# A two-layer graph kernel: small constants and later Wqk chunks on GpSimd's queue, pair 0's softmax in other space, and the last pair transposed by TensorE

## The chip, the core and the metric

The kernel runs on one core of a Trainium2 chip. TensorE (PE) does the matrix products, VectorE (DVE) and ScalarE (ACT) the elementwise work, GpSimd (POOL) and SyncE (SP) mostly start DMA transfers. The metric is the device time of one execution in microseconds. Before the change it is 2383.96 us, the median of 3 runs (2383.9 to 2384.36).

## What is computed

There are 128 independent graphs of 128 nodes with 512 features, all in float32. Two layers follow each other, each with a layer norm, a ReLU and a residual:

```python
# layer 0: h = relu(layernorm(x))
e = leaky_relu(sj[:, None, :] + si[:, :, None] + ab[0], 0.2)   # sj, si: projections of h
transition = A * exp(e) / (sum(A * exp(e), -1) + 1e-12)
H = sum over k of (Xk @ Wk[k] + bk[k]);  Xk = transition @ Xk    # k = 0, 1, 2
x = x + relu(H)
# layer 1: h = relu(layernorm(x))
q, k = split(h @ Wqk, 2);  v = h @ Wv
w = inv_scale * mask * sum(q * (adj @ (k * mask)), -1)
x = x + softmax(w, axis=nodes)[:, :, None] * v
```

## The kernel before

The graphs go through in 64 pairs (G = 2). Weights stay in SBUF. Both layers' products are seven Strassen products over blocks of the two graphs and two halves of the features (`strassen0`, lines 408 to 443, and `strassen1`, lines 445 to 472), so that the two large matrix products take 7/8 of the plain multiplications. Sums of weight blocks (`combine`, lines 193 to 199) are made once, sums of activation blocks (`left_sums`, line 385) once a pair. In layer 1, q never exists: `score_matrix` (lines 222 to 246) makes M = Wq Wk^T from eight chunks of Wqk that TensorE first transposes, four steps o = 0 to 3 with two chunks each.

The main loop (line 555) is a software pipeline over pairs. In turn p it runs layer 0's products of pair p, the propagation of pair p+1 (`propagate`, line 373), the norms of layer 1 for pair p and of layer 0 for pair p+2, layer 1's products of pair p-1, and the transpose of pair p's layer-1 input h2. A scheduler then orders each engine's instructions; an engine works through its own queue strictly in that order. At most eight transfers that SP and ACT start, and eight that GpSimd starts, are in flight, since each takes one of eight semaphores in turn and waits for the transfer that had it before.

The activations must stand transposed for the products. The kernel does this through memory: `by_blocks` (lines 296 to 304) writes h to DRAM (`hd`) and reads it back in 32-row blocks (`hv`), and `transposed` (line 306) lets DVE transpose 32x32 blocks, so that the features come in a permuted order (f, c, a) which the weights' rows follow.

The softmax over a graph's nodes needs the score column w as a row on all partitions. `spread_pair` (lines 312 to 327) does it by two small DMAs on GpSimd's queue (`pwd`, then `pw`), or for the last pair by TensorE (`spread`, line 115). `finish` (lines 492 to 510) then takes the maximum, the exponentials and the final multiply-add, and stores the pair. `end` (line 551) calls it for the pair before, in the middle of `strassen0`; in the last turn (p = 64), where there is no `strassen0`, it is called first of all (line 566), ahead of the last pair's layer-1 products.

At the start (lines 516 to 547) the norm of pair 0, the loading of pair 1, the row sums of Wv (`wv0_sums`, line 139), five small constants on SP's queue (lines 519 to 523), the score matrix, the layer-0 weight blocks (`stacked_weights`, line 204), the first attention and the first propagation follow each other. All eight Wqk chunks are started from ACT's queue (line 122), and `attention(0, ...)` uses the one-buffer tile `junk`, in which also every multiply-and-accumulate of DVE leaves its unwanted product.

Of the kernel before, what the change touches and what calls it, by code (L numbers as in the profile page):

```python
# [8 lines left out]
FP = mybir.dt.float32  # L9
AF = mybir.ActivationFunctionType  # L10
OP = mybir.AluOpType
# [4 lines left out]
def kernel(  # L16
# [55 lines left out]
    def load_x(p):  # L72
        s = slice(p * G, (p + 1) * G)
        xg[p] = loads.tile([P, G, D], FP, name="xg")
        nc.sync.dma_start(xg[p], x[s].rearrange("b n d -> n b d"))
        ag[p] = loads.tile([P, G, N], FP, name="ag")
        nc.sync.dma_start(ag[p], adj[s].rearrange("b n m -> n b m"))

# [37 lines left out]

        nc.tensor.transpose(dst, col.to_broadcast([P, P]), ident)

    def wqk_chunk(a, o):
        w = wpool.tile([P, DC, P], FP, name=f"w{a}")  # L120
        at = a * D + o * P
        nc.scalar.dma_start(w, wqk[:, at:at + P].rearrange("(c p) o -> p c o", p=P))
        return w

    nc.scalar.dma_start(awr, aw.rearrange("n o -> o n"))
    wchunks = {0: [wqk_chunk(a, 0) for a in range(2)]}
    for c in range(DC):
        nc.sync.dma_start(wv0_sb[c], wv0[c * P:(c + 1) * P])
    wchunks[1] = [wqk_chunk(a, 1) for a in range(2)]


    u_bc = const.tile([P, 2, D], FP, name="u_bc")
# [65 lines left out]
        nc.vector.tensor_sub(t[3], b21, t[1])  # L198
        return dict(zip((5, 6, 7, 4, 1, 2, 3), t + [b11, b21, b22]))

    bsum = const.tile([P, D], FP, name="bsum")
    blocks0, right0 = {}, {}

    def stacked_weights():
        blocks0["b11"] = block0(const, "b11", 0, 0)
        blocks0["b12"] = block0(None, "b12", 0, 1)
        blocks0["b22"] = block0(const, "b22", 1, 1)
        blocks0["b21"] = block0(const, "b21", 1, 0)

    def bias():  # L210
        pb = ps_t.tile([P, D], FP, name="pt")
# [10 lines left out]
    def score_matrix(o):  # L222

        if o == 0:
            pms.extend(ps_m.tile([P, D], FP, name="pm") for _ in range(DC))
        ws = wchunks.pop(o)
        wt = []
        for a in range(2):
            p = ps_t.tile([P, DC, P], FP, name="pt")
            for c in range(DC):  # L230
                nc.tensor.transpose(p[:, c, :], ws[a][:, c, :], ident)
            t = wpool.tile([P, D], FP, name=f"wt{a}")
            if a:
                nc.scalar.copy(t, p.rearrange("p c i -> p (c i)"))
            else:
                nc.scalar.copy(t.rearrange("p (f c a) -> p f c a", f=Q, c=DC),
                               p.rearrange("p c (f a) -> p f c a", f=Q))
            wt.append(t)
        if o + 2 < DC:
            wchunks[o + 2] = [wqk_chunk(a, o + 2) for a in range(2)]  # L240
        for c in range(DC):
            nc.tensor.matmul(pms[c], wt[0][:, c * P:(c + 1) * P], wt[1],
                             start=(o == 0), stop=(o == DC - 1))
            if o == DC - 1:
                for nh in range(2):
                    nc.scalar.copy(e[c // HC, nh][:, c % HC, 0, :], pms[c][:, nh * HD:(nh + 1) * HD])


    def norm_relu(src, name, pool):

        mv = small.tile([P, G, 2], FP, name="mv")
        for j in range(G):
# [13 lines left out]
        nc.vector.scalar_tensor_tensor(rs[:, 1], mean, -1.0, rs[:, 0], op0=OP.mult, op1=OP.mult)  # L266
        h = pool.tile([P, G, D], FP, name=name)
        for j in range(G):
            nc.scalar.activation(h[:, j, :], src[:, j, :], AF.Relu,  # L269
                                 bias=rs[:, 1, j:j + 1], scale=rs[:, 0, j:j + 1])  # L270
        return h

    cols = [const.tile([P, S32], FP, name=f"col{i}") for i in range(6)]
    for t in cols:
# [31 lines left out]
    def transposed(hv, dst):  # L306

        for j in range(G):
            nc.vector.transpose(dst[:, j].rearrange("p f (n b) -> p f n b", n=Q),  # L309
                                hv[:, j].rearrange("p n (f a) -> p f n a", f=Q))  # L310

    def spread_pair(col, name, by_dma):

# [131 lines left out]
    def strassen1(p, ahead):  # L445

        product = products(SX2.pop(p), R1)
        X2.pop(p)
        yv = late["p"].tile([P, G, 2, 2, HD], FP, name="yv")
        o = [[yv[:, j, nh].rearrange("p k d -> p (k d)") for nh in range(2)] for j in range(G)]  # L450
        s = late["p"].tile([P, 3, D], FP, name="s1")
        a, b, c = (ps_m.tile([P, D], FP, name="pm") for _ in range(3))
        product(a, 1, True)
        nc.scalar.copy(s[:, 0], a)
        product(b, 6, True)
        nc.vector.tensor_add(s[:, 1], b, s[:, 0])  # L456
        product(c, 7, True)
        agg = [aggregate(p, 0)]
        product(b, 5, False)
        nc.vector.tensor_add(s[:, 2], b, s[:, 0])  # L460
        nc.vector.tensor_add(o[1][1], c, s[:, 2])
        if ahead < NP:
            score_sums(ahead)
        product(a, 2, False)
        nc.scalar.copy(o[0][0], a)
        agg.append(aggregate(p, 1))
        H2.pop(p), AT.pop(p)
        product(b, 3, False)
        nc.vector.tensor_add(o[0][1], b, s[:, 0])
        product(c, 4, False)  # L470
        nc.vector.tensor_add(o[1][0], c, s[:, 1])
        return yv, scores(p, yv, agg)

    def aggregate(p, j):

        pa = ps_t.tile([P, D], FP, name="pt")
        nc.tensor.matmul(pa, AT[p][:, j, :], H2[p][:, j, :], start=True, stop=True)  # L477
        return pa

    def scores(p, yv, agg):  # L480

        w = cols[3 + p % 3]
        for j in range(G):
            junk = front.tile([P, D], FP, name="junk", bufs=1)
            b = p * G + j
            nc.vector.scalar_tensor_tensor(
                junk.rearrange("p (k d) -> p k d", k=2), agg[j].rearrange("p (k d) -> p k d", k=2),
                wscale[:, b:b + 1], yv[:, j, :, 0, :], op0=OP.mult, op1=OP.mult,
                accum_out=w[:, j:j + 1])
        return w  # L490

    def finish(peak, p, yv, ws, pw):


        w = ws[:, :6 * G].rearrange("p (k g) -> p k g", g=G)
        nc.vector.tensor_reduce(peak, pw, AX.X, OP.max, negate=True)
        for j in range(G):
            ej = front.tile([P, N], FP, name="ej")
            nc.scalar.activation(ej, pw[:, j, :], AF.Exp, bias=peak[:, j:j + 1],
                                 accum_out=w[:, 2, j:j + 1])  # L500
        nc.vector.tensor_add(w[:, 3], w[:, 0], peak)
        nc.scalar.activation(w[:, 4], w[:, 3], AF.Exp)
        nc.vector.reciprocal(w[:, 5], w[:, 2])
        nc.vector.tensor_mul(w[:, 3], w[:, 4], w[:, 5])
        x1 = X1.pop(p)
        for j in range(G):
            o = x1[:, j, :].rearrange("p (k d) -> p k d", k=2)
            nc.vector.scalar_tensor_tensor(o, yv[:, j, :, 1, :], w[:, 3, j:j + 1], o,  # L508
                                           op0=OP.mult, op1=OP.add)
        nc.sync.dma_start(out[p * G:(p + 1) * G].rearrange("b n d -> n b d"), x1)  # L510

    def begin(p):
        X[p] = front.tile([P, K, G, 2, HC, N], FP, name="x")
        transposed(HV.pop(p), X[p][:, 0].rearrange("p j h c n -> p j (h c) n"))

    norm0(0)
    load_x(1)
    wv0_sums()
    nc.sync.dma_start(bvc, bv0.rearrange("(p c) -> p c", c=DC))
    nc.sync.dma_start(awc, aw.rearrange("(a p c) o -> p a (c o)", a=2, c=DC))  # L520
    nc.sync.dma_start(ab_bc, bcast(ab, 0, 1))
    nc.sync.dma_start(bsum[:K], bk)
    nc.sync.dma_start(nm, nodemask)
    score_matrix(0)
    stacked_weights()
    score_matrix(1)
    attention_weights()
    masks()
    score_sums(0)
    score_matrix(2)  # L530
    attention(0, front.tile([P, D], FP, name="junk", bufs=1)[:, :G * N])
    score_matrix(3)
    bias()
    t_transposed(0)
    begin(0)
    propagate(0)
    prepare0(0)
    right0.update(combine(t=[const.tile([P, K, HC, HD], FP, name=f"t{i}") for i in range(1, 5)],
                          **blocks0))
    load_agb(0, X[0][:, 1, 0, 0, 0, 0:1])  # L540
    load_agb(1)
    transposed_adj(0)
# [12 lines left out]
    for p in range(NP + 1):  # L555
        if p < NP:
# [5 lines left out]
            strassen0(p, steps)  # L562
            if p + 1 < NP:
                propagate(p + 1)
        else:
            end()
        if p == 0:
            right1.update(combine(e[0, 0], e[0, 1], e[1, 0], e[1, 1], f))
            setup_ctx.close()
            R1 = {i: t.rearrange("p (s c) k o -> p s c (k o)", s=1) for i, t in right1.items()}  # L570
            late["p"] = ctx.enter_context(tc.tile_pool(name="late", bufs=1))
        if p < NP:
            H2[p] = norm_relu(X1[p], "h2", late["p"])
            hv2 = by_blocks(H2[p])
        if p + 2 < NP:
            norm0(p + 2)
        if p > 0:
            yv, w = strassen1(p - 1, p + 2)
        elif p + 2 < NP:
            score_sums(p + 2)  # L580
        if p + 1 < NP:
            prepare0(p + 1)
        if p > 0:
            ends.append((p - 1, yv, w, spread_pair(w, "pw", p < NP)))
        if p < NP:
            X2[p] = late["p"].tile([P, G, 2, HC, N], FP, name="x2")
            transposed(hv2, X2[p].rearrange("p j h c n -> p j (h c) n"))
            a = {(j, kh): X2[p][:, j, kh:kh + 1].rearrange("p k c n -> p k (c n)")
                 for j in range(G) for kh in range(2)}
            SX2[p] = left_sums(a, late["p"], "sx2", [1, HD])  # L590
    end()


# [23 lines left out]
```

## Time and profile before

| what | value |
|---|---|
| median time | 2383.96 us |
| span of the profiled execution | 2381.4 us |
| PE busy | 2343.4 us (98%) |
| DVE busy | 1828.5 us (77%) |
| ACT busy | 637.7 us (27%) |
| POOL busy | 374.3 us (16%) |
| DMA | 243.93 MB, mean 102 GB/s |

PE is busy in all but 38 us of the span. The page's second part, busy tenths in 40 slices, has PE at 9 in every slice but the first (8) and the last (6). The waits of PE in the first 80 us and in the last 40 us are views to read beside it, and the timeline around them. Two things help in reading. A wait is put down to the instruction that came last; behind a DVE instruction there may be another that held DVE's queue. And a matrix product of 128x512 in float32 is two records 0.43 us apart when the clock is full, so 0.86 us.

### The profile page before, as it was taken

How to read it: one execution, taken by the hardware profiler on the slowest of the kernel's cores; microseconds unless marked ns; L12 is line 12 of the kernel's file. 1: busy time of each engine (PE TensorE's matmuls, PEld its weight loads, DVE VectorE, ACT ScalarE, POOL GpSimd, SP SyncE). 2: the span in 40 equal slices, each digit the busy share in tenths (PEclk: the TensorE clock that was granted, in tenths of full speed). 3: DMA queues.
4: the chain of work that ended last, by engine and by line, in shares of the span. 5: the costliest groups of instructions: out<-in, count | busy, mean ns of one | idle time of the engine just before them, and what ended most of it. 6: DMA issues, size and time to landing. Idle time of an engine off the chain costs nothing.

```text
span 2381.4 us, 27851 instructions
## 1 busy us (share of the span) xinstructions
PE 2343.4 (98%) x8921; PEld 1660.8 (70%) x8921; DVE 1828.5 (77%) x4956; ACT 637.7 (27%) x1560; POOL 374.3 (16%) x653
## 2 busy tenths in 40 slices
PE   8999999999999999999999999999999999999996
PEld 5677677677677676676776776776776776766763
DVE  6787787887877877877877877878878778778764
ACT  3222222222222322322222222222223223223221
POOL 3111111111111111111111011111111111111100
PEclk9999999999999999999999999999999999999998
DMA  7334334344344344344343343343343443443421
GB/s 209 96 86 115 102 94 107 99 105 107 96 108 107 85 119 105 83 117 110 84 116 108 88 107 104 100 107 101 103 107 97 107 107 89 115 106 81 108 69 47
DMA packets 257357, 243.93 MB, mean 102 GB/s; under 512 B 28821, under 2 KB 182549, under 8 KB 257209
## 3 DMA queue, kind: packets, MB, share of 16 engines
q1 hardware_dynamic: 230150, 213.00, 31.6%
q0 software_dynamic: 22832, 27.05, 6.4%
q10 hardware_dynamic: 4226, 2.10, 0.3%
q8 instruction: 70, 1.15, 0.2%
q14 instruction: 79, 0.64, 0.1%
HBM read 141.25 MB, written 100.79 MB: 102 GB/s over the span
## 4 chain that ended last, share of the span: by engine, by line
PE 90%; DVE 3%; DMA 2%; issue 1%; ACT 0%; POOL 0%; DVEq 0%; POOLq 0%; ACTq 0%
PE pm L402 75%; PE pt L381 8%; PE pt L477 4%; PE pt L369 1%; DMA pwd<-pwt 1%; PE pt L365 1%; DMA pw<-pwd 1%; DVE st L254 0%; DMA pz<-pzd 0%; DVE junk L292 0%; DMA pzd<-pzt 0%; DVE x L309 0%; DVE x L442 0%; DVE x L508 0%; DVE sx L390 0%
## 5 line engine op out<-in xcount | busy, mean ns | idle before, releaser
L402 PE MATMUL pm<-t,sx 128*128 128x256 f32 x2304 | 507.9, 379 | 3.4 <-DVE sx L389 3.4
L402 PEld LDWEIGHTS pm<-t,sx 128*128 128x128 f32 x2304 | 437.6, 190 | 63.7 <-DVE sx L389 4.2
L402 PE MATMUL pm<-b,x 128*128 128x256 f32 x1536 | 363.0, 379 | 0.0
L402 PE MATMUL pm<-f,sx 128*128 128x512 f32 x768 | 353.1, 595 | 1.7 <-DVE s L456 1.6
L402 PEld LDWEIGHTS pm<-b,x 128*128 128x128 f32 x1536 | 282.1, 190 | 59.6 <-issue 29.7
L320 POOL DMA_DIRECT2D pzd<-pzt x124 | 69.0, 559 | 1411.1 <-DVE pzt L317 1411.0
L402 PEld LDWEIGHTS pm<-f,sx 128*128 128x128 f32 x768 | 146.1, 191 | 187.1 <-issue 162.7
L402 PE MATMUL pm<-e,x 128*128 128x512 f32 x512 | 243.2, 597 | 13.5 <-DVE x L309 13.5
L383 ACT COPY x<-pt 128x512 f32<-128x512 f32 x256 | 147.6, 577 | 367.8 <-PE pt L381 367.7
L381 PE MATMUL pt<-tt,h 128*128 128x256 f32 x1024 | 231.6, 379 | 0.5 <-ACT tt L370 0.5
L292 DVE SCALAR_TENSOR_TENSOR junk<-h,u_bc 128x512 f32<-128x512 f32 x256 | 177.2, 692 | 66.3 <-ACT h L269 52.9
L381 PEld LDWEIGHTS pt<-tt,h 128*128 128x128 f32 x1024 | 194.5, 190 | 27.5 <-ACT tt L370 1.1
L402 PE MATMUL pm<-b,sx 128*128 128x256 f32 x768 | 176.2, 379 | 0.0
L402 PE MATMUL pm<-t,x 128*128 128x256 f32 x768 | 176.2, 379 | 0.0
L402 PEld LDWEIGHTS pm<-e,x 128*128 128x128 f32 x512 | 97.6, 191 | 110.4 <-issue 91.0
L309 DVE STREAM_TRANSPOSE x<-hv 128x512 f32<-128x512 f32 x256 | 166.3, 688 | 5.6 <-DMA hv<-hd 3.7
L337 ACT ACTIVATE s<-s 128x256 f32<-128x256 f32 x63 | 26.3, 417 | 511.3 <-DVE s L335 511.3
L402 PEld LDWEIGHTS pm<-b,sx 128*128 128x128 f32 x768 | 145.9, 190 | 19.8
L402 PEld LDWEIGHTS pm<-t,x 128*128 128x128 f32 x768 | 145.9, 190 | 19.8
L87 POOL DMA_DIRECT2D agb<-in_adj_dram x256 | 153.3, 603 | 21.1 <-issue 13.1
L269 ACT ACTIVATE h<-xg,rs 128x512 f32<-128x512 f32 x128 | 97.3, 808 | 173.7 <-DVE rs L266 173.7
L477 PE MATMUL pt<-h,aT 128*128 128x512 f32 x256 | 130.6, 592 | 0.0
(131 smaller groups left out, 2807.6 us busy)
## 6 DMA issues: line engine op xcount, KB each, us to landing
hd<-h SPq DMA_DIRECT2D x128, 512.0 KB, 4.0
hv<-hd SPq DMA_DIRECT2D x512, 128.0 KB, 5.3
xg<-in_x_dram SPq DMA_DIRECT2D x64, 512.0 KB, 3.6
out_dram<-x SPq DMA_DIRECT2D x64, 512.0 KB, 2.8
ag<-in_adj_dram SPq DMA_DIRECT2D x64, 128.0 KB, 2.7
agb<-in_adj_dram POOLq DMA_DIRECT2D x256, 32.0 KB, 4.0
pw<-pwd POOLq DMA_DIRECT2D x63, 128.0 KB, 3.3
pz<-pzd POOLq DMA_DIRECT2D x62, 128.0 KB, 5.6
```

What stands on the lines that cost most here:

```text
L87: nc.gpsimd.dma_start(agb[p][c * S32:(c + 1) * S32].rearrange("p g q i -> p (g q) i"), v[c])
L269: nc.scalar.activation(h[:, j, :], src[:, j, :], AF.Relu, bias=rs[:, 1, j:j + 1], scale=rs[:, 0, j:j + 1])
L292: nc.vector.scalar_tensor_tensor(junk, h[:, j, :], 1.0, u_bc[:, a, :], op0=OP.mult, op1=OP.mult, accum_out=s[:, a * G + j:a * G + j + 1])
L309: nc.vector.transpose(dst[:, j].rearrange("p f (n b) -> p f n b", n=Q), hv[:, j].rearrange("p n (f a) -> p f n a", f=Q))
L320: nc.gpsimd.dma_start(d[j], t[j::S32])
L337: nc.scalar.activation(ex, z, AF.Exp)
L365: nc.tensor.transpose(pt[:, j, :], t[:, j, :], ident)
L369: nc.tensor.matmul(pt[:, j, :], t[:, j, :], tt[:, j, 0, :], start=True, stop=True)
L381: nc.tensor.matmul(pt[:, c].rearrange("p k n -> p (k n)"), h[:, j, at:at + P], tt[:, j].rearrange("p k n -> p (k n)"), start=True, stop=True)
L383: nc.scalar.copy(X[p][:, 1:3, j, kh].rearrange("p k c n -> p c k n"), pt)
L402: nc.tensor.matmul(bank[:, :r.shape[-1]], left[i][:, k, c * P:(c + 1) * P], r, start=(first and at == 0), stop=(at == len(chunks) - 1), sk ...
L477: nc.tensor.matmul(pa, AT[p][:, j, :], H2[p][:, j, :], start=True, stop=True)
```

## The change

Five edits go together.

1. **Loads at the start.** The five small constants (bv, aw as columns, ab, the biases, the node mask) are started from GpSimd's queue at the very beginning instead of from SP's queue. The Wqk chunks of steps 2 and 3 also go to GpSimd's queue. Pair 0's adjacency is loaded after Wv.
2. **Order at the start.** Pair 1's x is loaded, and so normed, later: between layer 0's blocks b22 and b21 instead of ahead of `wv0_sums`. The blocks b12, b22 and b21 are loaded after the first score sums in the program's order.
3. **Space.** `attention(0, ...)` works in a corner of two not yet written weight sums (now one tile `tw`) instead of `junk`.
4. **The last pair's transpose.** Its h2 is written unpermuted by ACT, and TensorE transposes it with eight 128x128 transposes into PSUM, copied out by ACT (graph 0) and DVE (graph 1). The products that read h2 directly take it through a permuted view.
5. **The last turn.** `end` for pair 62 moves into `strassen1(63)`, behind its fourth product. The last pair is scored, finished and stored graph by graph, the first graph ahead of the seventh product in the program.

```diff
@@ load_x
-        ag[p] = loads.tile([P, G, N], FP, name="ag")
-        nc.sync.dma_start(ag[p], adj[s].rearrange("b n m -> n b m"))
+        if p > 0:
+            load_ag(p)
@@ setup
-    wchunks = {0: [wqk_chunk(a, 0) for a in range(2)]}
+    wchunks = {0: [wqk_chunk(a, 0, nc.scalar) for a in range(2)]}
     for c in range(DC):
         nc.sync.dma_start(wv0_sb[c], wv0[c * P:(c + 1) * P])
+    load_ag(0)
+    nc.gpsimd.dma_start(bvc, bv0.rearrange("(p c) -> p c", c=DC))
+    nc.gpsimd.dma_start(awc, aw.rearrange("(a p c) o -> p a (c o)", a=2, c=DC))
+    nc.gpsimd.dma_start(ab_bc, bcast(ab, 0, 1))
...
+    nc.gpsimd.dma_start(bsum[:K], bk)
+    nc.gpsimd.dma_start(nm, nodemask)
+    wchunks[1] = [wqk_chunk(a, 1, nc.scalar) for a in range(2)]
@@ score_matrix
-            wchunks[o + 2] = [wqk_chunk(a, o + 2) for a in range(2)]
+            wchunks[o + 2] = [wqk_chunk(a, o + 2, nc.gpsimd) for a in range(2)]
@@ new
+    def transposed_by_pe(h, dst):
...
+        for j in range(G):
+            pt = ps_t.tile([P, DC, P], FP, name="pt")
+            for f in range(Q):
+                nc.tensor.transpose(pt[:, f, :], h[:, j, f * P:(f + 1) * P], ident)
+            (nc.vector.tensor_copy if j else nc.scalar.copy)(dst[:, j], pt)
@@ strassen1
         nc.vector.tensor_add(o[1][1], c, s[:, 2])
...
+        if p == NP - 1:
+            end(s[:, 2, :G])
         product(a, 2, False)
...
+        w = cols[3 + p % 3]
+        if p == NP - 1:
+            last(p, yv, w, agg, 0)
         product(c, 4, False)
         nc.vector.tensor_add(o[1][0], c, s[:, 1])
-        return yv, scores(p, yv, agg)
+        if p == NP - 1:
+            last(p, yv, w, agg, 1)
+            return
...
+    def last(p, yv, w, agg, j):
...
+        score(p, yv, w, agg, j)
+        pw = ps_t.tile([P, DC, P], FP, name="pt")
+        spread(pw[:, j, :], w[:, j:j + 1])
+        finish(small.tile([P, G], FP, name="peak"), p, yv, w, pw[:, :G], slice(j, j + 1))
@@ setup order
     norm0(0)
-    load_x(1)
     wv0_sums()
-    nc.sync.dma_start(bvc, bv0.rearrange("(p c) -> p c", c=DC))
...
     score_matrix(0)
-    stacked_weights()
+    blocks0["b11"] = block0(const, "b11", 0, 0)
     score_matrix(1)
     attention_weights()
     masks()
     score_sums(0)
+    blocks0["b12"] = block0(None, "b12", 0, 1)
+    blocks0["b22"] = block0(const, "b22", 1, 1)
+    load_x(1)
+    blocks0["b21"] = block0(const, "b21", 1, 0)
     score_matrix(2)
-    attention(0, front.tile([P, D], FP, name="junk", bufs=1)[:, :G * N])
+    tw = const.tile([P, 4, K, HC, HD], FP, name="t")
+    at = K * HC * HD - N
+    attention(0, tw.rearrange("p i k c o -> p (i k c o)")[:, at:at + G * N])
@@ main loop
-            H2[p] = norm_relu(X1[p], "h2", late["p"])
-            hv2 = by_blocks(H2[p])
+            H2[p] = norm_relu(X1[p], "h2", late["p"], p == NP - 1)
+            if p + 1 < NP:
+                hv2 = by_blocks(H2[p])
...
-            transposed(hv2, X2[p].rearrange("p j h c n -> p j (h c) n"))
+            hT2 = X2[p].rearrange("p j h c n -> p j (h c) n")
+            if p + 1 < NP:
+                transposed(hv2, hT2)
+            else:
+                transposed_by_pe(H2[p], hT2)
```

## The prediction

> **What bounds the kernel now.** First the page: PE is busy 2343.4 of 2381.4 us, and in the chain that ended last 90% is PE. So every engine but PE matters only where PE waits for it, and all of PE's idle time is 38 us. The busy tenths put it at the two ends. I then read the waits of PE at each end, and the chain of the last 60 us.
>
> The waits of PE (us in total, times, longest), first from 0 to 80 us, then from 2340 us to the end:
>
> ```profile
> PE pm L402 <- DVE sx L389: 3.4, 2, 2.7
> PE pt L117 <- DVE junk L292: 2.9, 1, 2.9
> PE pt L143 <- DMA f<-in_L_gnn_aw_dram: 2.4, 1, 2.4
> PE pt L231 <- DMA w<-in_L_gnn_Wqk_dram: 1.6, 1, 1.6
> PE pt L117 <- DVE junk L148: 1.1, 1, 1.1
> PE pm L242 <- ACT wt L234: 1.0, 1, 1.0
> ...
> PE pm L402 <- DVE x L309: 11.4, 1, 11.4
> ```
>
> At the end one wait stands out: the last pair's first product waits 11.4 us for DVE's transpose of the block-wise copy `hv`. The chain over that stretch (start, us, what) shows what held DVE:
>
> ```profile
> 2345.60 0.22 DVE pwt L317
> ...
> 2346.10 0.56 POOL pwd L320
> 2346.66 2.85 DMA pwd<-pwt
> ...
> 2350.07 3.19 DMA pw<-pwd
> ...
> 2353.74 0.89 ACT ej L499 x4
> ...
> 2356.53 0.63 DVE x L309
> 2357.16 0.04 issue
> 2357.20 14.97 PE pm L402 x28
> ```
>
> It is not only the round trip of h2. `hv` was started from 2345.03 to 2346.83 and lands a median 5.3 us later (DMA issues), about 2352. But pair 62's finish stands ahead of the transpose in DVE's queue and waits for its own two DMAs until 2353.28. Both waits must go, and the change touches both.
>
> At the start, DVE and ACT are what PE waits for, and the timeline shows what they wait for:
>
> ```profile
> 13.16 1.29 DVE L254 BATCH_NORM_STATS2 st<-xg 128x6 f32<-128x512 f32 x2 [4.69 <-DMA xg<-in_x_dram]
> 16.48 0.59 ACT L236 COPY wt<-pt 128x512 f32<-128x512 f32 x1 [5.64 <-DMA ag<-in_adj_dram]
> 19.04 0.17 DVE L159 SCALAR_TENSOR_TENSOR awc<-awc,bvc 128x4 f32<-128x4 f32 x1 [3.99 <-DMA awc<-in_L_gnn_aw_dram]
> ```
>
> DVE loses 4.7 us to pair 1's x and 4.0 us to a small constant (10.1 us from issue to landing). ACT loses 5.6 us because it is itself starting Wqk chunks (its DMA issues last from 10.68 for 5.76 us) with PSUM copies queued behind.
>
> **What the Trainium skill says.** (1) "TensorE: Matmul & The Clock Gate", Part 1: after an idle window of about 3.4 us PE runs at half clock, and needs about 3.4 us of work to get back. The trace agrees: after the 11.4 us wait the weight loads come 0.85 us apart instead of 0.43. (2) Same page, Part 4: a PE transpose does 128x128 at once into PSUM, a copy must follow, and transposes don't count as work for the clock. The trace shows the duration (273 ns median at L365, 0.11 us apart), not the last. (3) "DMA: Bandwidth & Descriptors", Anatomy of one DMA: about 2 us fixed, whatever the size. Here `pwd`, with almost no bytes, took 2.85 us. (4) "Trainium Kernel Development and Optimization", Key Constraints: queues of SP, ACT and POOL share the same 16 DMA engines; another queue saves only issue time. So part 1 can move waits, not bytes; DMA is 84%, over 100% and 92% busy in the first three windows of 10 us.
>
> **The end, step by step** (in the clock of before; PE's order is read from the built program: pair 62's product 4, eight transposes, aggregate of graph 0, products 1, 6, 7, 5, 2, aggregate of graph 1, products 3, 4).
> - Pair 62's product 4 gives way to the next at 2343.88. h2 is ready earlier (ACT 2340.65 + 1.52). Eight transposes at 0.11 us: 0.9 (at half clock 1.9; I take 0.9). PE to 2344.8.
> - Aggregate 0.86, product 1 two matmuls, 1.72: to 2347.4. ACT's copy of graph 0 (0.59, as other PSUM copies) ends about 2345.1 and is hidden.
> - DVE's copy of graph 1 is no row of before; DVE's nearest PSUM read of 128x512 is 0.69, bounds 0.6 to 0.75. It is queued behind the scores of pair 62, so 2345.6 to 2346.3, then `pwt` 0.2 and three sums of 0.43: 2347.85. Product 6 waits about 0.5 us.
> - Products 6, 7, 5, 2: 6.9, aggregate 0.86, products 3 and 4: 3.4. PE ends at 2359.1. Before, DVE took up the last product at 2372.19, that is 13.1 us later. Of these 11.4 are the wait and some 2.6 the half clock after it (six matmul records 0.43 longer), less the transposes.
> - Unpermuted writing of h2 and permuted reading of h2 by two aggregates: ACT's copies with 32-element runs (L236, 586 ns) cost what plain ones do (L234, 589 ns), so 0 for ACT, hidden anyway. No row shows PE reading so; 0 to 1.7 us (a doubling), I take 0.
> - Added wait: pair 62's finish now stands in DVE's queue after product 5. `pwt` is 0.7 later, so `pw` is there at 2354.0; DVE comes to it at 2354.7 (product 5 ends 2353.1, two adds). ACT's exponentials stand behind the copy of product 2 (2355.0 to 2355.6) and end about 2356.7; two multiply-adds of 0.7 end at 2358.5. Behind them wait product 3's add and score 0 (0.69 + 0.75) and only then product 4's add: about 2360.0 instead of 2359.1. So 0.9 us of the gain goes here.
> - Tail: before, from that add (2372.19) to the last multiply-add's end (2377.33) 5.1 us. Now add, max of graph 0 (0.26), score 1 (0.75), spread 0.35, max 0.26, exponentials 0.8, graph 0's multiply-add in their shadow, small steps 0.4, graph 1's 0.7: about 4.5 us, to 2364.5. The store was 4.07 us from there to the end; half the bytes, by the loads of 128 and 512 KB (2.7 and 3.6 us) 0.4 less: 3.7. End 2368.2.
> - Sum: 2381.4 - 2368.2 = 13.2 us, bounds 11.5 (double reads, half-clock transposes) to 14.2 (no queueing at 62's finish).
>
> **The start, step by step.**
> - ACT no longer starts chunks, so the wt copies of step 1 come at about 12 instead of 16.48. PE's wait of 1.0 goes: step 1's products end 20 instead of 21.2.
> - DVE's eight row sums (0.75 each) start at 7.77 and no longer have the two waits: about 15 instead of 23.5. u_bc is ready at about 21.4 (before 26.97), score 0 at 21.8, and PE's waits of 1.1 and 2.9 shrink to about 0.3. The clock also stays up. PE reaches the transposes of t at about 33 instead of 39.4.
> - But pair 1's norm (BN 1.3, small steps), and the sums of weights (4 x 1.75), are still DVE's, now between t (about 28) and the first activation sums. Four score sums of pair 1 are put between these (0.75 each), and ACT's copies of the propagation wait for its norm. I get the second sum at 43.7 (before 48.07). So 4.4 us there, not 6.
> - Pair 1's attention then comes after the score sums and one 1.2 us weight sum, t at 53.3, while PE is there at 51.7: 1.6 back. The later waits (2.7 at L389, 2.1 at L309 near 91 us) stay: they are DVE's work per turn, not what was moved. Net 2.9 us, bounds 0.5 and 6 (all of PE's advance kept).
> - Constants on GpSimd: five issues of about 0.6 us at 1 to 5 us, behind them the chunks of step 2, the gate of b11, the chunks of step 3 and the other six Wk loads, each waiting for the one eight before. Even with 10 us of landing awc is there at 12; its instructions stand third in DVE's queue, behind them the other six row sums, which would then end at 16.5 instead of 15, still ahead of PE's 20. Wk's last blocks start at about 17 instead of 12.5 and are used at 30 and later: 0. The new space of `attention(0)`: frees DVE's `junk`, 0 by itself.
> - Steady state: each engine's order is the same for pairs 2 to 61, so 0.
>
> **Sum.** 13.2 + 3.0 = 16.2; 2383.96 - 16.2 = 2367.7 us.
>
> **Rivals.**
> - R1, the start gives nothing: DVE or a late load takes the place of the waits removed. For: DVE is 75 to 90% busy from 20 to 40 us, and DMA is full until 30. Against: 8.7 us of DVE's idle time there are pure waits. Only the end is kept: 2383.96 - 13.2 = 2370.8.
> - R2, PE's whole advance at the start is kept: 2383.96 - 13.2 - 6 = 2364.7. Against: pair 1's norm must still be done by DVE ahead of the same sums.
> - R3, slower: the five small transfers land one after another at 10.1 us each, since all chunks and Wk loads queue behind them on GpSimd. The mask would come near 52 us, where PE wants it at 24: 2383.96 + 28 - 13.2 = 2398.8. Against: before, three of them in flight together took 10 us together.
> - R4, no difference: the finish of pair 62 inside the last turn meets late DMAs and puts PSUM copies off by some 9 us: 2383.96 - 13.2 + 9 = 2379.8. Against: `pw` has 8.4 us between its transpose and its use, where before 7.7 were needed.
>
> **Chances.** As worked out 0.70, R1 0.15, R2 0.11, R3 0.02, R4 0.02. So faster 0.96, same 0.02, slower 0.02. The range takes in R1 and R2 with the bounds of the costs at the end: 2363.0 to 2372.2.
>
> **What would show it.** Right: PE has no wait over 1 us after 2340 us; the last matmul ends about 13 us earlier from the span's end of before, less the start's gain; pair 62's max sits after product 5's adds; awc is waited for by under 2 us; the first `sx`-wait of PE is over at about 44 us. Wrong: a wait of PE for `hv`'s successor x, aggregates longer than 0.86, GpSimd's chunks landing after 23 us, or other times in the middle pairs.

## The result, and the profile after

| kernel | median us | lowest to highest | ratio to before, 95% interval |
|---|---|---|---|
| before | 2384.16 | 2381.78 to 2389.9 (6 runs) | 1 |
| changed | 2366.66 | 2365.77 to 2370.26 (6 runs) | 0.9925 [0.9913, 0.9938] |

The change takes 17.5 us off. 2367.7 was predicted, between 2363.0 and 2372.2. The profiled execution of the changed kernel took 2370.26 us (span 2368.5), the longest of its six, so its profile shows less of the gain than the median does. PE is busy 2342.0 us of it (99%), before 2343.4 (98%): the change took idle time, not work.

**The end.** PE's waits from 2320 us to the end, where before one wait of 11.4 us stood (us in total, times, longest):

```profile
PE pt L122 <- DVE col L544: 1.2, 1, 1.2
PE pt L122 <- DVE junk L526: 0.5, 1, 0.5
```

Both belong to the last pair's spread of its scores, behind the products. No product waits for half a microsecond or more. The chain over the same stretch (start, us, what):

```profile
2342.51 3.43 PE pm L421 x8
2345.95 0.87 PE pt L328 x8
2346.82 0.86 PE pt L519 x2
2347.68 8.73 PE pm L421 x20
...
2358.29 1.42 DVE x L549 x2
2359.70 0.61 DVE x L493
2360.32 0.02 issue
2360.34 0.76 DVE junk L526 x2
2361.10 0.60 DVE x L498
...
2364.56 0.75 DVE x L549
```

The eight transposes (L328) take 0.87 us together, the aggregate (L519) that reads h2 through the permuted view takes 0.86 as before, and 20 product records follow in 8.73 us at full clock. Then DVE ends the kernel: pair 62's multiply-adds (the two at L549) and only behind them the last product's add (L498).

To compare the ends of two executions I count from the moment at which pair 62's product 4 gives way: 2343.88 us before, 2345.78 in the changed kernel. From there to the end it was 37.5 us before and is 22.7 now. So the end gives 14.8 us in the profiles. The other side of this is that the changed kernel's profiled execution comes to pair 62 1.9 us *later* than before: in this execution the start gives nothing.

**The start.** PE's waits from 0 to 80 us:

```profile
PE pt L236 <- DMA w<-in_L_gnn_Wqk_dram: 4.1, 2, 3.9
PE pm L421 <- DVE sx L408: 2.9, 2, 2.0
PE pt L155 <- DMA f<-in_L_gnn_aw_dram: 2.3, 1, 2.3
PE pm L247 <- ACT wt L239: 1.7, 1, 1.7
PE pt L122 <- DVE junk L303: 0.7, 1, 0.7
PE pt L400 <- ACT tt L389: 0.5, 1, 0.5
PE pt L384 <- DVE t L365: 0.3, 1, 0.3
```

The waits for DVE's row sums and scores (`junk`, 2.9 and 1.1 before) are down to 0.7, as meant. But the wait for the second Wqk chunk of step 0 has grown from 1.6 to 3.9 us. The timeline shows where it starts, and what DVE then waits for:

```profile
10.26 0.15 DVE L171 SCALAR_TENSOR_TENSOR awc<-awc,bvc 128x4 f32<-128x4 f32 x1
11.01 1.97 PE L236 MATMUL pt<-ident,w 128*128 128x128 f32 x8 [3.88 <-DMA w<-in_L_gnn_Wqk_dram]
22.79 0.16 DVE L176 TENSOR_TENSOR cz<-pt,ab_bc 128x1 f32<-128x1 f32 x1 [8.01 <-PE pt L175]
30.36 0.71 DVE L320 STREAM_TRANSPOSE x<-hv 128x512 f32<-128x512 f32 x1 [3.85 <-DMA hv<-hd]
47.45 1.13 PE L421 MATMUL pm<-t,sx 128*128 128x256 f32 x4 [1.97 <-DVE sx L408]
90.81 3.78 PE L421 MATMUL pm<-e,x 128*128 128x512 f32 x4 [3.27 <-DVE x L320]
```

`awc` is not waited for at all. The chunk is there at 11.01, against 8.85 before. DVE is done with the row sums at 14.8 us and then idles 8.0 us, since PE's score matrix, started late, comes to `cz` only then. The first product with an activation sum starts at 47.45 (before 48.13), pair 0's first layer-1 product at 90.81 (before 91.49). The lead is 0.7 us in both places, and even that is lost next: the wait ahead of the product at 90.81 is 3.27 us (before 2.09), the clock is at half from 90.05 to 96.88 us, so for 6.1 us of the work behind that wait (before for 3.4 us), and the next pair's t is waited for by 1.2 us (before 0.4). 0.7 - (6.1 - 3.4)/2 - 0.8 = -1.45 us. Some turns of the loop that take longer than the others, of which more below, add 0.4: together they make the 1.9 us by which pair 62 comes later.

### The profile page after: what moved, and what is told of

Same layout as the page of the kernel before. It is cut to its first block, busy times and chain, and to the rows that moved or that the text cites. A ratio compares the mean times of both kernels' runs of the same rounds, so it can differ in the third digit from the quotient of the medians.

```text
span 2368.5 us, 27872 instructions
## 1 busy us (share of the span) xinstructions
PE 2342.0 (99%) x8929; PEld 1660.0 (70%) x8929; DVE 1825.3 (77%) x4959; ACT 637.5 (27%) x1562; POOL 379.0 (16%) x662
## 4 chain that ended last, share of the span: by engine, by line
PE 89%; DVE 4%; DMA 2%; issue 1%; ACT 1%; POOL 0%; DVEq 0%; POOLq 0%
PE pm L421 75%; PE pt L400 8%; PE pt L519 4%; DMA pwd<-pwt 1%; PE pt L388 1%; PE pt L384 1%; DMA pw<-pwd 1%; DVE st L260 0%; DMA pz<-pzd 0%; DVE junk L303 0%; DVE x L461 0%; DVE x L320 0%; DVE x L549 0%; DMA pzd<-pzt 0%; DVE sx L409 0%
## 5 line engine op out<-in xcount | busy, mean ns | idle before, releaser
L320 DVE STREAM_TRANSPOSE x<-hv 128x512 f32<-128x512 f32 x254 | 165.1, 688 | 10.8 <-DMA hv<-hd 9.7
L519 PE MATMUL pt<-h,aT 128*128 128x512 f32 x256 | 130.7, 592 | 0.0
```

Of the source, the lines that this page charges most:

```text
L519: nc.tensor.matmul(to, AT[p][:, j, :], h2, start=True, stop=True)
```

## Experiments

All kernels are made from the changed one. Each was measured beside runs of the kernel before on the same chip, and each gain below is against those. None leaves out any of the computation.

### The end: both edits, and each by itself

Three kernels keep the start of before. `e1_end_only` has edits 4 and 5; `e3_pe_transpose_only` only the transpose by TensorE, with the last turn as before; `e4_finish_only` only the new last turn, with h2 of the last pair through DRAM as before. Edits undone, with `AT_START` standing for edits 1 to 3:

```diff
@@ e1, e3, e4: AT_START undone
-    load_ag(0)
-    nc.gpsimd.dma_start(bvc, bv0.rearrange("(p c) -> p c", c=DC))
...
+    load_x(1)
     wv0_sums()
+    nc.sync.dma_start(bvc, bv0.rearrange("(p c) -> p c", c=DC))
...
@@ e3: the last turn as before
-        if p == NP - 1:
-            end(s[:, 2, :G])
...
-            last(p, yv, w, agg, 1)
-            return
+        return yv, scores(p, yv, agg)
@@ e4: the last pair's h2 through DRAM
-                transposed_by_pe(H2[p], hT2)
+                transposed(hv2, hT2)
```

> The kernel before with edits 4 and 5 alone (last pair transposed by TensorE, pair 62's finish inside the last turn, last pair finished graph by graph); the start is that of before. My theory (the end gives 13 to 15 us, the start some 3): 13.2 us by the prediction's sum, 14.8 us by the two profiles counted from pair 62's last product to the end; so about 2369.5 us where before has 2384, and some 3 us slower than the whole change. Rival R1 (the start gives nothing): as fast as the whole change, 2366.7 us within 1 us.

> The kernel before with edit 4 alone: the last pair's h2 is transposed by TensorE, but pair 62's finish stays at the head of the last turn and the last pair is finished whole. By the order of DVE's queue the finish comes behind product 6's add, so TensorE is held only once, ahead of product 4, until pair 62's multiply-adds are through (the same yv buffer). I expect 12 us less than before, 2372 us, with one wait of about 1.3 us of TensorE for a DVE add. Rival (both waits must go, as the prediction said: the finish waits for its DMAs ahead of what TensorE needs): only 4 to 8 us less.

> The kernel before with edit 5 alone: pair 62's finish inside the last turn, last pair finished graph by graph, but h2 of the last pair still goes through DRAM. The products then start when the block-wise copy has landed, about 8 to 9 us after pair 62's last product instead of 13.3, still at half clock. I expect 5.3 us less than before, 2378.7 us: 4.3 from the wait, 1 from the tail. Rival (the round trip of h2 alone is the 11.4 us, DVE's queue adds nothing): 1 us less, 2383 us.

| kernel | median us | gain us | ratio |
|---|---|---|---|
| e1, both | 2367.93 | 15.3 | 0.9937 [0.9925, 0.9950] |
| e3, transpose by TensorE | 2369.44 | 13.8 | 0.9947 [0.9933, 0.9960] |
| e4, the last turn | 2373.71 | 9.5 | 0.9968 [0.9956, 0.9981] |

The end is worth 15.3 us by the times too. But the two edits are not two halves of it: alone they give 13.8 and 9.5 (I had expected 12 and 5.3), together 15.3, so they take away largely the same thing. "Both waits must go" is wrong in the sense in which I used it: with the DRAM trip gone and `end` called first in the last turn, as before, PE waits nowhere over 1.3 us. DVE's queue in e3 shows why (timeline of e3, DVE and PE):

```profile
2348.83 0.69 DVE L500 TENSOR_TENSOR s<-pm,s 128x512 f32<-128x512 f32 x1 [1.69 <-PE pm L442]
2351.97 0.42 DVE L557 TENSOR_REDUCE peak<-pw 128x2 f32<-128x256 f32 x1 [2.44 <-DMA pw<-pwd]
...
2353.80 1.42 DVE L570 SCALAR_TENSOR_TENSOR x<-yv,col,x 128x512 f32<-128x512 f32 x2
2355.26 0.69 DVE L505 TENSOR_TENSOR yv<-pm,s 128x512 f32<-128x512 f32 x1
2356.00 0.48 PEld L442 LDWEIGHTS pm<-f,x 128*128 128x128 f32 x2 [0.38 <-DVE yv L505]
```

Pair 62's maximum (`peak<-pw`) still waits 2.44 us for its DMA, but it stands behind product 6's add (L500), and what PE needs next from DVE comes in time: the product that follows waits 0.38 us. Once DVE no longer has to transpose blocks, the finish ahead of it in the queue has nothing behind it that PE needs soon.

In e4 the DRAM trip is still there, and its wait can be read by itself (timeline of e4):

```profile
2340.12 0.38 SPq L331 DMA_DIRECT2D hd<-h  x1
2342.96 1.80 SPq L335 DMA_DIRECT2D hv<-hd  x4
2347.41 1.30 DVE L341 STREAM_TRANSPOSE x<-hv 128x512 f32<-128x512 f32 x2 [3.68 <-DMA hv<-hd]
2348.18 2.05 PE L442 MATMUL pm<-e,x 128*128 128x512 f32 x2 [4.50 <-DVE x L341]
```

The write takes 2.8 us (2340.12 to 2342.96), the last of the four reads is issued by 2344.76 and DVE takes up the data at 2347.41, under 3 us later. So of the 11.4 us that PE waited before, about 4.5 were the trip and some 7 were pair 62's finish in DVE's queue. I had `hv` landing at 2352 from a median of 5.3 us over the whole execution. Here it is half that.

### The start by itself

`e2_start_only` has edits 1 to 3 and the end of before:

```diff
-            if p + 1 < NP:
-                hv2 = by_blocks(H2[p])
+            hv2 = by_blocks(H2[p])
...
-        if p == NP - 1:
-            end(s[:, 2, :G])
```

> The kernel before with edits 1, 2 and 3 alone; the end is that of before. My theory: about 3 us faster than before, 2381 us. R1: no difference, 2384 us within 1 us, since TensorE's advance at the first products (1.9 us in the profile of the changed kernel) is lost at pair 0's layer-1 product, where it waited 3.3 us instead of 2.1. R2 (the whole advance kept): 6 us faster, 2378 us.

2378.02 us, 5.2 us less than before, ratio 0.9978 [0.9970, 0.9985], so 3.6 to 7.1 us. The start does give something, in the measure of the prediction's 3.0 or a bit more. The other way to get it, the whole less the end, gives less: the change's 17.5 less e1's 15.3 is 2.2. With intervals of some 3 us on each of these two the answers don't contradict each other; 2 to 5 us is all that can be said. The profiled executions don't narrow it. Pair 3's first layer-1 product comes at 204.3 us in e2, 206.6 in e9 (the changed kernel once more, see below) and 207.7 in the changed kernel; with the start of before it comes at 206.2 (before), 206.2 (e4), 206.7 (e1) and 207.0 (e3).

### The parts of the start

Since the profile of the change shows so little of the start's gain, these kernels add one part of the start to the whole end. `e5_end_and_queues`: constants and later chunks on GpSimd's queue, but loads, order and space as before. `e6_end_and_order`: the new order, the late adjacency and the space `tw`, but constants on SP's queue in their old place and chunks on ACT's.

```diff
@@ e5: the order as before
-    load_ag(0)
...
+    load_x(1)
     wv0_sums()
...
@@ e6: the queues as before
-    nc.gpsimd.dma_start(bvc, bv0.rearrange("(p c) -> p c", c=DC))
...
+    nc.sync.dma_start(bvc, bv0.rearrange("(p c) -> p c", c=DC))
...
-            wchunks[o + 2] = [wqk_chunk(a, o + 2, nc.gpsimd) for a in range(2)]
+            wchunks[o + 2] = [wqk_chunk(a, o + 2, nc.scalar) for a in range(2)]
```

> The changed kernel without edits 2 and 3 and with pair 0's adjacency loaded first again: of the start only the other queues are left (five constants and the Wqk chunks of steps 2 and 3 on GpSimd). The end alone gave 15.3 us less than before, the whole change 17.5 in its own comparison. My theory (ACT's 5.6 us and DVE's 4.0 us of waits were the queues' part, but DVE still waits for pair 1's x ahead of the row sums): 1 to 2 us beyond the end alone, about 17 us less than before. Rival (the queues are all of the start's gain): the same as the whole change within 1 us. R1 (nothing at the start counts): 15 us less than before.

> The changed kernel with the constants back on SP's queue (behind the row sums in the program) and all Wqk chunks back on ACT's: of the start only the order, the space and the later adjacency are left. My theory (each part takes away one of two waits in a row, so each gives little alone): 1 to 2 us beyond the end alone, 16.5 us less than before. Rival (the constants' 10 us of landing set TensorE's start): 15 us less than before or worse.

e5: 2362.19 us, gain 20.4, ratio 0.9915 [0.9901, 0.9929]. e6: 2363.6 us, gain 19.0, ratio 0.9921 [0.9909, 0.9934]. Both are more than I expected (17 and 16.5). By the medians each half of the start, put to the end, gives more than both halves do (17.5), though the intervals overlap. PE's waits in e5, from 0 to 80 us, name a difference:

```profile
PE pt L257 <- DMA w<-in_L_gnn_Wqk_dram: 4.2, 4, 1.8
```

Its longest wait for a chunk is 1.8 us, and e6's is 1.7. A wait depends on when PE comes to the chunk, too: in e5 PE comes at 8.4 us, in the changed kernel at 7.1. So here are, over all runs, the longest wait for a chunk (it is always for step 0's second) and, in brackets, when PE takes the chunk up, both in us:

| start | kernels: wait (taken up at) |
|---|---|
| constants late, order of before | before 1.6 (8.85), e1 2.7 (9.79), e3 2.9 (9.98), e4 2.1 (9.22) |
| constants late, new order | e6 1.7 (8.80) |
| constants early, order of before | e5 1.8 (10.22), e12 3.0 (10.09) |
| constants early, new order (the change) | change 3.9 (11.01), e2 5.1 (12.50), e8 4.7 (12.18), e9 4.6 (11.82) |
| constants behind the chunk, new order | e7 1.4 (8.55), e10 2.3 (9.42), e11 2.1 (9.63) |

The chunk is latest where constants start early in the new order. Early constants in the order of before bring it little later than late ones do there (10.1 and 10.2 us against 8.9 to 10.0), and the new order with late constants not at all (8.80).

In e6 DVE waits 7.6 us for `awc` instead, and the time hardly minds.

### The chunk: constants held back, and the change again

`e7_constants_gated` is the changed kernel with one difference: GpSimd starts the five constants only when the second Wqk chunk has landed. Each of their tiles first gets a small copy out of this chunk:

```diff
+    for t in (bvc, awc[:, 0], ab_bc, bsum, nm):
+        nc.gpsimd.tensor_copy(t[:, 0:1], wchunks[0][1][:, 0, 0:1])
     nc.gpsimd.dma_start(bvc, bv0.rearrange("(p c) -> p c", c=DC))
```

`e9_change_again` is the changed kernel itself, with no edit, on another chip than in the first comparison: it asks whether the whole change is really slower than e5.

> The changed kernel, but GpSimd starts the five constants only when the second Wqk chunk has landed (five one-element copies from that chunk as gates). In the profile of the changed kernel TensorE waits 3.9 us for that chunk, to 11.0 us, in the kernel before 1.6 us, to 8.9 us. Theory A (the constants' many small descriptors share the DMA engines and delay the chunk): the wait falls back to under 2 us and the kernel is 1 to 2 us faster than the changed one, 2365 us. Theory B (the chunk is late for another cause, the weight-block rows that SP starts earlier): the wait stays at 4 us, the time the same as the changed kernel's or, if the constants come too late for DVE, 1 to 3 us slower.

> The changed kernel once more, on the same chip as the three below: its 17.5 us less than before came from another comparison, while its parts, measured apart, gave 15.3 (the end), 20.4 (the end and the queues) and 19.0 (the end and the order). Theory C (the three start edits together delay the second Wqk chunk, to 11 us and later, so that the whole is 2 to 3 us slower than the end with the queues alone): 17 to 18 us less than before. Rival (a difference between comparisons only): 20 us less than before.

e7: 2361.11 us (2359.49 to 2363.86), gain 21.5, ratio 0.9908 [0.9893, 0.9923], the lowest median of all kernels. e9: 2364.95 us, gain 17.9, ratio 0.9923 [0.9911, 0.9934], as the change the first time (0.9925). PE's timeline in e7 and then in e9:

```profile
8.55 1.11 PE L260 MATMUL pt<-ident,w 128*128 128x128 f32 x4 [1.41 <-DMA w<-in_L_gnn_Wqk_dram]
11.73 5.51 PE L271 MATMUL pm<-wt,wt 128*128 128x512 f32 x9
```

```profile
11.82 3.22 PE L257 MATMUL pt<-ident,w 128*128 128x128 f32 x12 [4.58 <-DMA w<-in_L_gnn_Wqk_dram]
```

The chunk is there at 8.55 us with the constants held back and at 11.82 without: the five small transfers, 76.5 KB in all, cost a transfer of 256 KB about 3 us. The busy share of the DMA engines in tenths and the bytes moved, per fortieth of the first 30 us (0.75 us each), show the same, first in the changed kernel, then in e7:

```profile
DMA  0047999997139999989999988999999999999999
GB/s 0 0 107 205 396 358 350 372 367 214 38 140 343 343 346 380 273 201 230 370 366 341 294 214 290 380 411 344 167 169 225 276 296 285 285 273 315 276 225 193
```

```profile
DMA  0048999999999999899589668999999999999999
GB/s 0 0 98 232 366 368 358 354 378 397 364 343 349 357 204 273 314 399 267 127 287 306 200 163 219 269 244 286 236 229 275 320 343 348 285 369 352 360 365 289
```

In the changed kernel the rate falls to 214, 38 and 140 GB/s between 6.8 and 9 us, with the chunk still on its way. In e7 there is no such gap before 10 us. All kernels divide so: from 6.75 to 9.75 us the slowest slice has 38 to 223 GB/s in the six with early constants (178 and 223 in e5 and e12, with the order of before) and 313 or more in the other eight. The gap is not one of DMA engines busy with the constants, for their busy share falls with the rate, to 0.1 at the lowest; what they stand still for isn't shown.

With the gap gone, e7's PE reaches the transposes of t at 33.36 us (change 37.41; I had predicted 33), its first product with an activation sum starts at 43.40 (change 47.45, e9 47.25, before 48.13; I had predicted 43.7), and pair 0's first layer-1 product at 86.33 instead of 90.81. The step of the prediction was right for a start without this delay. The delay and what it does to the start are shown by e7, and once more by two kernels that come below, e10 (constants held back) beside e8: the chunk at 9.42 and 12.18, the first product with an activation sum at 44.42 and 47.45. That e7 as a whole is faster than the change is not proven. The two gains differ by 3.6 us, but the intervals overlap ([0.9893, 0.9923] against [0.9913, 0.9938] and e9's [0.9911, 0.9934]), and e10 has a median gain only 0.7 us above e8's.

### The wait near 90 us

I took pair 0's first layer-1 product to wait for h2's trip through DRAM as the last pair's did. `e8_pair0_h2_by_pe` gives pair 0 what the change gives to the last pair. `e10_gated_and_pair0_h2` is e8 with the constants held back as in e7, `e11_gated_pair0_both` also lets GpSimd reorder pair 0's layer-0 h so that TensorE transposes it too, and `e12_queues_and_pair0_h2` is e5 with pair 0's h2 by TensorE.

```diff
@@ e8, e10, e11, e12
-            if p + 1 < NP:
-                transposed(hv2, hT2)
-            else:
+            if p in (0, NP - 1):
                 transposed_by_pe(H2[p], hT2)
+            else:
+                transposed(hv2, hT2)
@@ e11: and pair 0's layer-0 h
+            nc.gpsimd.tensor_copy(unpermuted(HV[p][:, j, :]), h[:, j, :].rearrange("p (c f a) -> p c f a", c=DC, f=Q))
```

> The changed kernel, with pair 0's layer-1 input h2 also transposed by TensorE instead of through DRAM. In the profile of the changed kernel TensorE waits 3.3 us for that block-wise copy near 91 us and then runs 6.8 us at half clock; in the kernel before 2.1 us and 3.4 us. My theory (the start's advance is lost at this wait and at the half clock behind it): the wait is gone, no half clock near 91 us, 3 to 5 us less than the changed kernel, about 2362 us. Rival (DVE's work, not the copy, holds TensorE there): the wait only moves by some microseconds, within 1 us of the changed kernel.

> The changed kernel with both single edits that helped in its profile: constants gated by the second Wqk chunk's landing (alone 21.5 us less than before) and pair 0's h2 transposed by TensorE (alone 17.8 less, TensorE's wait for x near 90 us gone). If their gains add: 23 to 25 us less than before, 2359 us. Rival (with the advance of the gate, DVE is what pair 0's layer 1 waits for, and the second edit gives nothing more): 21 to 22 us less.

> The kernel of e10, and pair 0's layer-0 input too is transposed by TensorE (GpSimd writes a reordered copy, no trip through DRAM), so that attention's DVE queue no longer waits for that block-wise copy (3.8 us in the profile of the changed kernel) and 1 MB less is moved in the first 30 us. Theory: 1 to 3 us less than e10. Rival (GpSimd's two slow copies delay the Wqk chunks of step 2 and the weight blocks behind them): 1 to 4 us more than e10.

> The end, the queues and pair 0's h2 by TensorE, without the new order, space and adjacency (e5 with e8's edit). If the wait for x near 88 us (2.2 us in e5) goes and nothing takes its place: 22 us less than before. Rival: DVE takes its place, 20 us less as e5.

| kernel | median us | gain us | ratio |
|---|---|---|---|
| e8 | 2364.86 | 17.8 | 0.9927 [0.9914, 0.9939] |
| e10 | 2364.36 | 18.5 | 0.9919 [0.9906, 0.9932] |
| e11 | 2364.96 | 17.9 | 0.9917 [0.9904, 0.9929] |
| e12 | 2368.07 | 14.8 | 0.9937 [0.9925, 0.9950] |

All four miss what I expected of them, and e8 comes out as its rival said. The timeline of the changed kernel has the reason, which I had overlooked (SP's and DVE's rows):

```profile
77.19 4.04 SPq L314 DMA_DIRECT2D hv<-hd  x8
87.01 0.60 DVE L353 TENSOR_SCALAR s<-pz,col,cz 128x128 f32<-128x128 f32 x2 [4.18 <-DMA pz<-pzd]
90.05 1.30 DVE L320 STREAM_TRANSPOSE x<-hv 128x512 f32<-128x512 f32 x2
```

The last of the block-wise reads `hv` is started at 80.8 us, and none takes more than 3.8 us to land, so h2 is there by 84.6. But DVE waits 4.18 us, to 87.01, for `pz`, the row of pair 2's attention scores that GpSimd's small DMAs bring, then works through that pair's attention with one pause of 0.5 us, and comes to the transpose only at 90.05. It is DVE's queue behind `pz` that PE waits for, not h2's trip. In e8 PE's wait for h2 is gone, and so is the half clock after it. Yet the gain is that of the change. PE's waits in e8, from 80 to 2330 us:

```profile
PE pm L443 <- DVE s L501: 2.1, 3, 0.9
PE pt L406 <- DVE t L387: 1.6, 1, 1.6
```

DVE takes up `pz` at 87.44 us in e8 and is 9.24 of 10 us busy from 88 to 98: PE now waits 1.6 us for t, which stands in the same queue, where in the changed kernel it waited 3.3 for x and 1.2 for t.

e12 fell below e5, from which it differs by that edit alone, and e10 below e7. To see where, I split the profiled executions in three: the start, to pair 3's first layer-1 product; the 58 turns of the loop from there to pair 61's; and the rest, which is 68.1 to 68.4 us in every kernel with both edits of the end (before 83.1). Most turns take 35.98 us in every profile, but in each execution some take longer, by up to 2.7 us. In us:

| profiled execution | start | sum of what turns take beyond 35.98 |
|---|---|---|
| before | 206.2 | 5.0 |
| change | 207.7 | 5.4 |
| e9, the change again | 206.6 | 2.9 |
| e8 | 202.6 | 4.8 |
| e7 | 201.5 | 5.2 |
| e10 | 199.1 | 9.0 |
| e11 | 201.6 | 6.2 |
| e5 | 202.6 | 3.1 |
| e12 | 204.3 | 8.0 |

At the start, then, the edit of pair 0's h2 does help: e8 is 4 to 5 us ahead of the two executions of the change, and e10 is 2.4 ahead of e7. A part of that is the clock, which is at half for 10.2 us between 20 and 110 us in the change, for 6.8 in e9, 3.4 in e7 and never in e8 and e10. The longer turns take the lead of e10 away, 3.8 us more than in e7. e12 loses 4.9 us to e5 in them, and 1.8 at the start: its first product with an activation sum is already late, at 49.30 against 46.12.

The longest such turn, in e10 near 1316 us, has this wait of PE:

```profile
PE pm L446 <- DVE s L504: 2.1, 1, 2.1
```

and in it GpSimd's wait for the small transfer `pwd` is 7.0 us, where the kernel before has 5.0 between 1316 and 1356 us (its `pwd` lands a median 5.4 us after the issue). The longer turns are not scattered by chance alone. In all four kernels with this edit the longest is the one from pair 34 to pair 35 (1.5 to 2.7 us), in before, e1, e3, e4 and e6 the one from pair 36 to pair 37 (1.5 to 2.4 us). What makes them, and whether the edit adds to them, these runs don't tell.

## Why the prediction came out as it did

**Total.** 16.2 us predicted, 17.5 measured, 17.9 with e9. The end gave more than its term. The start's term is right in size as far as the times can tell, but what I worked out for it did not happen in the changed kernel. That the sum came so close is in part luck.

**The end, 13.2 us; measured 14.8 in the profiles and 15.3 in e1.** The order was right: transposes, aggregate, products, pair 62's maximum behind product 5's adds (its row is at 2356.16, 10.4 us after product 4; my 2354.7 was 10.8). Counted from the moment when product 4 gives way:

| step | predicted | measured |
|---|---|---|
| eight transposes | 0.9 | 0.9 |
| product 6 starts | 4.0, with a wait of 0.5 | 3.5, no wait |
| last product's add (L498) | 16.1 | 15.2 |
| last multiply-add ends | 20.6 | 19.5 |
| end of the span | 24.3 | 22.7 |

The mis-sized terms are DVE's copy and sums ahead of product 6 (no wait at all, 0.5 us), the adds behind pair 62's finish (0.4), small steps after them (0.2) and the store (3.2 us against 3.7): together the 1.6 us. The queueing behind pair 62's finish was seen rightly: in the chain L549 stands ahead of L493 and L498. PE's permuted read costs nothing, as I took it (0.86 us for the aggregate).

**"Both waits must go"** is the step that failed in its reasoning. e3 (13.8) shows that the transpose by TensorE does it almost alone. e4 (9.5) shows that the queueing behind pair 62's finish was the larger part of the 11.4 us, about 7. The sum was right because it was worked out for the two edits together.

**The start, 3.0 us; measured 2 to 5.** Three steps failed. (1) "Constants on GpSimd" were costed at nothing, because I looked at when they land and who needs them, and not at what they do to the load that lands beside them: step 0's second chunk came 2.2 us later in the change (11.01 against 8.85), and 3 us later in e9 than in e7. From the Trainium skill, "Trainium Kernel Development and Optimization", Key Constraints, I had even quoted that the queues share the same 16 DMA engines; the conclusion that part 1 moves no bytes left out that it moves them *in front of* something. (2) "PE reaches the transposes of t at about 33 instead of 39.4": it was 37.41. The chunk was late, and `hv` of pair 0, for which DVE waited 3.85 us to 30.36, held up ACT's next copy and with it PE, by 1.7 us; 3.4 us of half clock came on top. In e7 that wait for `hv` is gone too, and PE is there at 33.36. (3) "The later waits stay": the one near 91 us grew to 3.3 in the profiled execution. Its reason, "they are DVE's work per turn", was right, and e8 was built as if it were not; what the reckoning left out is the half clock behind the wait. What was right: ACT's copies are no longer held up, DVE's row sums end at 14.8 (predicted 15), `awc` is not waited for, and a turn of the loop takes 35.98 us as before, apart from the longer ones that both kernels have.

**The rivals.** R1 (start worth nothing, 2370.8) is what the profiled execution shows, at 2370.26 us. By e2, 5.2 us for the start alone, it is not what the change does; the median of six alone couldn't tell, since the end by itself gives 15.3 of its 17.5. R2 (2364.7) needs the whole advance of PE at the start; e7, with 43.40 us at the first activation sum, comes closest to it (4.7 us ahead of before there). R3 and R4 did not happen: `pw` is there in time, and no small constant was late.

**Open.** How much the start gives within 2 to 5 us; which of the five constants delays the chunk, what the DMA engines stand still for in the gap, and why the new order makes it worse; whether e7 is faster than the change; what makes the longer turns in which e10 and e12 lose.

## What to carry to other kernels

Ask of every transfer that is moved earlier not only who waits for it but which large load is then on its way, and hold small ones back until that load has landed: here 76.5 KB of constants delayed a chunk of 256 KB by 3 us (that holding them back pays in the whole time is not proven). When a wait follows a slow transfer *and* stands behind other work in an engine's queue, the two overlap: cost each removed alone, since one edit may take away most of both. When a wait is put down to an engine, look first at what that engine itself waited for: `pz` stood in front of h2's transpose, and the transfer blamed had landed over 5 us earlier. And before saying that two gains don't add up, split the time into start, turns and end: e10's start was the shortest of all, and the turns behind it took the lead away.

## What was not expected of the hardware

**The half clock after a short wait comes or doesn't.** The Trainium skill, "TensorE: Matmul & The Clock Gate", Part 1, has TensorE at half clock after at least one idle window of about 3.4 us. It calls this window "free-running", and says that the moment at which the clock changes depends on where in it the first product lands. Here shorter waits were enough, and the same kernel met one with and without the half clock. Ahead of pair 0's first layer-1 product PE waited 2.1 us in the kernel before, and the clock was then at half for 3.4 us (92.75 to 96.16 us). In the changed kernel it waited 3.3 us, and the clock was at half for 6.8 us (90.05 to 96.88). In e9, the same program, it waited 2.3 us there and kept its full clock; e9 had been at half for 6.8 us earlier, from 46.57 to 53.40, around two waits for DVE of 1.4 and 2.0 us. Windows of the changed kernel (busy us and count of PE, PEld, DVE, ACT, POOL, then PE's clock, DMA share, GB/s), then of e9:

```profile
92.00:94.00 2.00, 2.00 (x4) 0.83 (x3) 2.00 (x8) 0.00 (x0) 0.00 (x0) 0.50 0.00 0
94.00:96.00 2.00, 2.00 (x3) 0.57 (x2) 1.97 (x5) 0.59 (x1) 0.00 (x0) 0.50 0.05 8
```

```profile
92.00:94.00 2.00, 1.95 (x4) 0.64 (x4) 2.00 (x6) 0.02 (x1) 0.00 (x0) 1.00 0.00 0
94.00:96.00 2.00, 1.81 (x6) 0.86 (x7) 1.97 (x8) 0.94 (x2) 0.00 (x0) 1.00 0.00 0
```

So one and the same wait costs about 0, 1.7 or 3.0 us beyond itself (half of the time that PE works at half clock), which is as much as the start's whole gain. It may be a part of why executions of the changed kernel differ by 4 us.

**A few small transfers make a gap in a full stream.** In the changed kernel 38 GB/s for 0.75 us where some 350 went before and after, with the DMA engines 0.1 busy, while a 256 KB load was still out.
